# A decoder in one launch: one expert step taken up after two batches' routing, and its inner products queued in two groups

## The chip, the cores and the metric

The kernel runs on one core of a Trainium2 chip. The metric is the device time of one execution in microseconds (us); lower is better. Everything is in float32 except some small counting and quantised products in bfloat16.

## The reference, cut to what matters

Input x is 4 batches of 256 tokens with 256 features; a context of 4 x 1601 rows goes with it. Six sublayers follow each other, each ending in a residual and a layer norm: windowed attention, cross attention over the context, a quantised gated network, a causal attention with 16 heads, a linear cross attention with a gate, and last a mixture of eight experts. The change is about that last one:

```python
logits = 30 * tanh(x @ w_gate / 30)          # x is 1024 x 256, w_gate 256 x 8
probs = softmax(logits)
_, idx = top_k(probs, 2)
weights = probs * one_hot(idx).sum(-2)
for e in range(8):                            # w1, w3: 256 x 512, w2: 512 x 256
    h = silu(x @ w1[e]) * (x @ w3[e])
    out = out + h @ w2[e] * weights[:, e:e+1]
x = layernorm(x + out)
```

Each token needs two of the eight experts.

## The kernel before, in words

**Order.** The function `decoder` does not emit instructions as it goes. Each call records an operation with its inputs, outputs, assumed durations and a priority (`at_prio`) in a `Loom`. At the end, `weave` takes the operations one by one: among those whose inputs are done and whose buffers have room, the one that can start earliest by the planner's own durations goes next, and the priority breaks ties. So the order on every engine is written out by that planner, and the chip then runs each engine's queue strictly in that order, waiting where an input is late. A `piece` is a group of TensorE instructions that the planner places as one.

**Routing.** The expert sublayer does not run all tokens through all experts. For each batch, `route` finds the two experts of each token, counts how many tokens each expert has so far (`nxt`), and GpSimd scatters each token's row, with its gate and its slot, into a list in DRAM that is sorted by expert (`lists`, `scatter`). The last batch, batch 3, is routed in two halves of 128 tokens.

**Steps.** The work on the lists is done in steps of 128 rows of one expert. Which expert and which rows a step takes is known only on the chip: `tile_table` computes it with some 25 small VectorE instructions from the counts in `nxt`, and writes a table `tab` of expert numbers and row numbers. There is one table behind the routing of three batches (five steps), one behind that and the first half of the last batch (two more), and one at the end (16 steps, of which 13 always run and 3 only if the counts call for them). `EARLY` holds how many full steps the counts guarantee at each point, whatever the tokens choose.

**One step** (`expert_tile`, line 1436 and after), with the names used below, k being the number of the step in order:

- fetch: SyncE reads the row number from the table and loads 128 rows, `xg`, from `lists` (129 KB, line 1443).
- weights: SyncE reads the expert number and loads `wt`, w1 and w3 of the expert, in two transfers of 512 KB (line 1455). There are four `wt` buffers.
- T: TensorE transposes `xg` in two instructions of the program; ScalarE or VectorE copies the result to `xgT`.
- W: 16 products of `wt` with `xgT`, eight for w1 (first group, here Wa) and eight for w3 (second group, Wb). A product shows as two MATMUL records in the profile.
- ScalarE takes the tanh of the first group into `eh`. VectorE multiplies it with the first group (`eh<-eh,bank`), and then with the second group (`eh<-bank,eh`).
- Y: four products of `eh` with `w2e`, the resident w2 of all experts.
- VectorE scales the result (`ey`) and computes slot numbers; GpSimd scatters the rows to `yd` in DRAM. The last two steps are added up in PSUM with one-hot matrices (`pick`) instead, on top of the residual and of what `yd` holds (`entry`, `back`), and `finish` normalises and writes the output.

The buffers `xgT`, `eh` and `ey` of the steps lie in a pool, `p6`, of the scope `work`, which opens only when the scope `causal` is closed, that is when the causal attention of the last batch is done.

**The end of the routing.** `l1_attention` of batch 3 yields its two halves one after the other, each followed by `l1_cross` and `route`; the tables and the steps are recorded between them:

```python
if b == B - 1:
    at_prio(8)
    n = EARLY[ts[0]]
    tab, taken = tile_table(n, taken)
    for i in range(n):
        expert_tile(i, tab, level)
```

`ts[0]` is 0 for the first half (and for whole batches) and 1 for the second. `level` counts how many routings a step has to wait for: a fetch of a step is ordered only behind the scatters of lower levels.

## Time and profile before

| what | value |
|---|---|
| median of 3 runs | 690.63 us (690.26 to 690.64) |
| the profiled execution, its own time | 690.3 us |
| span of its profile, first to last instruction | 688.6 us |
| TensorE busy | 656.5 us, 95% of the span |
| VectorE, ScalarE, GpSimd busy | 444.0, 296.2, 120.7 us |
| mean granted TensorE clock | 0.985 of full speed |
| DMA | 85.36 MB, mean 124 GB/s |

The 1.7 us between the profiled execution's time and its span lie outside the first and last instruction. The times in the profile are from this one execution; its own time is 0.3 us under the median of the runs. An engine's busy share is an average over stages with different limits, and idle time of an engine that nothing waits for costs nothing. All helper calls of VectorE, ScalarE and GpSimd have one line, 408, and all products line 271, so rows are told apart by their tiles. "PE" is TensorE, "PEld" its weight loads, "DVE" VectorE, "ACT" ScalarE, "POOL" GpSimd, "SP" SyncE.

### The profile page before, as it was taken

The page shows a single profiled execution, that of the slowest core. Times are in us where ns is not written, and L with a number is a line of the kernel's source. Part 1 is how long each engine was busy: PE and PEld are TensorE (multiplying, and loading weights), DVE is VectorE, ACT ScalarE, POOL GpSimd, SP SyncE. Part 2 cuts the span into 40 slices and gives each one's busy share as a digit, 9 for nine tenths or more (in the row PEclk, how much of TensorE's full clock was granted, in tenths as well). Part 3 has the DMA queues.
Part 4 walks back from the last instruction along what each step waited for, and adds up shares of the span by engine and source line. Part 5 has one row for each costly group of instructions (what it writes and reads, how often), then busy time and mean ns, then how long its engine had stood idle before and what let it go on. Part 6 is the DMA issues. An engine that isn't in the chain of part 4 may idle for free.

```text
span 688.6 us, 12316 instructions
## 1 busy us (share of the span) xinstructions
PE 656.5 (95%) x4385; PEld 524.3 (76%) x4389; DVE 444.0 (64%) x1152; ACT 296.2 (43%) x930; POOL 120.7 (18%) x166
## 2 busy tenths in 40 slices
PE   9999999999999999999989999999997899999992
PEld 6778788678877777777667677777765799899991
DVE  6899887433526844464699997777688466434353
ACT  4779766211132423334347777656445312111101
POOL 3331132122300000000022101141203213121102
PEclk9999999999999999999999999999999899999996
DMA  9932121537998422000010340000000582895432
GB/s 307 363 96 63 45 66 40 177 100 236 335 340 307 146 96 96 0 1 1 1 54 1 105 142 1 1 32 1 31 1 21 207 277 73 295 339 217 146 130 69
DMA packets 62463, 85.36 MB, mean 124 GB/s; under 512 B 4462, under 2 KB 45812, under 8 KB 62388
## 3 DMA queue, kind: packets, MB, share of 16 engines
q1 hardware_dynamic: 60756, 79.96, 34.9%
q0 software_dynamic: 1632, 4.48, 1.8%
q8 instruction: 38, 0.62, 0.4%
q14 instruction: 37, 0.30, 0.1%
HBM read 67.29 MB, written 17.13 MB: 123 GB/s over the span
## 4 chain that ended last, share of the span: by engine, by line
PE 83%; DVE 10%; ACT 4%; POOL 1%; issue 1%; ACTq 0%; POOLq 0%; DVEq 0%
PE bank L271 74%; PE bank L278 9%; ACT at L408 3%; DVE at L408 2%; DVE nm L408 2%; DVE x L408 1%; POOL rstd L408 1%; DVE st L408 0%; DVE h L408 0%; DVE fm L408 0%; DVE as L408 0%; DVE kf L408 0%; ACT fm L408 0%; DVE back L408 0%; DVE bank L408 0%
## 5 line engine op out<-in xcount | busy, mean ns | idle before, releaser
L408 ACT ACTIVATE at<-at,nm 128x128 f32<-128x128 f32 (+1 forms) x256 | 106.4, 419 | 22.6 <-DVE nm L408 21.7
L271 PE MATMUL bank<-xgT,wt 128*128 128x128 f32 x640 | 75.9, 280 | 0.6 <-DVE xgT L408 0.5
L271 PEld LDWEIGHTS bank<-xgT,wt 128*128 128x128 f32 x640 | 75.2, 196 | 1.7 <-DVE xgT L408 0.8
L278 PE MATMUL bank<-ident,at 128*128 128x128 f32 (+1 forms) x440 | 61.4, 277 | 2.0 <-DVE at L408 1.8
L278 PEld LDWEIGHTS bank<-ident,at 128*128 128x128 f32 (+1 forms) x440 | 50.7, 142 | 14.2 <-issue 7.1
L271 PE MATMUL bank<-V,aT 128*128 128x256 f32 (+1 forms) x240 | 55.1, 380 | 0.6 <-DVE o L408 0.6
L271 PE MATMUL bank<-KT,qT 128*128 128x512 f32 (+1 forms) x128 | 54.7, 554 | 0.0
L271 PEld LDWEIGHTS bank<-V,aT 128*128 128x128 f32 (+1 forms) x240 | 45.3, 190 | 10.5 <-issue 3.6
L271 PE MATMUL bank<-kf,V 128*128 128x256 f32 (+1 forms) x208 | 50.0, 382 | 1.1 <-DVE kf L408 1.1
L408 POOL TENSOR_SCALAR rstd<-mv 128x2 f32<-128x2 f32 (+1 forms) x26 | 5.8, 222 | 258.5 <-DVE mv L408 186.2
L408 DVE TENSOR_REDUCE nm<-at 128x4 f32<-128x512 f32 (+1 forms) x64 | 50.6, 809 | 0.4
L271 PE MATMUL bank<-wkv,KT 128*128 128x256 f32 (+1 forms) x208 | 49.6, 382 | 0.0
L408 ACT ACTIVATION_READ_ACCUMULATOR at<-at,nm 128x1 f32 x256 | 48.6, 190 | 0.0
L271 PEld LDWEIGHTS bank<-kf,V 128*128 128x128 f32 (+1 forms) x208 | 38.6, 190 | 7.2 <-DVE kf L408 2.3
L271 PEld LDWEIGHTS bank<-wkv,KT 128*128 128x128 f32 (+1 forms) x208 | 38.0, 186 | 6.9 <-issue 1.0
L408 ACT COPY aT<-bank 128x512 f32<-128x512 f32 (+2 forms) x58 | 30.6, 554 | 26.6 <-PE bank L278 25.8
L408 ACT ACTIVATE eh<-bank 128x512 f32<-128x512 f32 x20 | 11.9, 597 | 66.5 <-PE bank L271 66.5
L408 DVE TENSOR_REDUCE m<-bank 128x1 f32<-128x512 f32 (+1 forms) x32 | 20.5, 640 | 29.7 <-PE bank L271 29.7
L408 DVE TENSOR_TENSOR at<-at,rs 128x512 f32<-128x512 f32 (+1 forms) x44 | 38.4, 873 | 1.0
L408 POOL TENSOR_TENSOR at<-at,rs 128x512 f32<-128x512 f32 (+1 forms) x20 | 22.8, 1141 | 87.9 <-DVE rs L408 80.7
L408 ACT ACTIVATE fm<-bank 128x512 f32<-128x512 f32 (+2 forms) x33 | 17.8, 550 | 46.6 <-PE bank L271 46.1
L271 PE MATMUL bank<-w2e,eh 128*128 x160 | 37.8, 380 | 0.0
(268 smaller groups left out, 1243.2 us busy)
## 6 DMA issues: line engine op xcount, KB each, us to landing
wt<-in_w SPq DMA_DIRECT2D x40, 512.0 KB, 5.0
lists<-h SPq DMA_DIRECT2D x6, 1548.0 KB, 17.9
KT<-in_ctxT SPq DMA_DIRECT2D x6, 1024.0 KB, 6.9
V<-in_ctx SPq DMA_DIRECT2D x6, 1024.0 KB, 6.0
w2e<-in_w SPq DMA_DIRECT2D x8, 512.0 KB, 8.7
KT<-in_ctxT SPq DMA_DIRECT2D x6, 577.0 KB, 5.1
V<-in_ctx SPq DMA_DIRECT2D x6, 512.0 KB, 4.2
xg<-lists SPq DMA_DIRECT2D x20, 129.0 KB, 4.2
```

What stands on the lines that cost most here:

```text
L271: lambda: self.nc.tensor.matmul(real(o), real(lhsT), real(rhs), start=real(start), stop=stop, **kw)
L278: fns.append(lambda: self.nc.tensor.transpose(real(o), real(x), real(ident)))
L408: return getattr(engine, method)(*[real(x) for x in args], **{k: real(x) for k, x in kw.items()})
```

## The change

There are two edits.

First, `EARLY` gets a third entry: how many full steps the counts guarantee behind the first two batches. By the formula that is one: 2 x 512 token-expert pairs less 8 x 127, divided by 128 and rounded up. The guaranteed steps are now 1, 4 and 2 in place of 5 and 2, so their sum, and the 16 of the last table, stay the same. The loop makes a table and its steps from batch 2 on (`b >= B - 2`): one step is recorded before batch 2 is routed, with a table of its own, and it is ordered only behind the scatters of batches 0 and 1.

Second, the 16 products W of a step are recorded as two pieces of eight, first group and second group, with half the assumed duration each, in place of one piece. The instructions are the same; the planner may now put other TensorE work between the groups, and it sees the first group end earlier.

```diff
-    EARLY = [-(-(2 * n - NE * (P - 1)) // P) for n in (3 * S, T - P)]
-    EARLY[1] -= EARLY[0]
+    EARLY = [-(-(2 * n - NE * (P - 1)) // P) for n in (2 * S, 3 * S, T - P)]
+    EARLY = [EARLY[0], EARLY[1] - EARLY[0], EARLY[2] - EARLY[1]]
...
         h = pool.tile((P, EI // P, P), F32, "eh")
         pa = [bank((P, EI // P, P)), bank((P, EI // P, P))]
-        with piece(3.52, [h], what="tile"):
-            for j in range(2):
+        for j in range(2):
+            with piece(1.76, [h], what="tile"):
                 for m in range(EI // P):
                     for c in range(2):
                         mm(pa[j][:, m], wt[:, j, c, m * P : (m + 1) * P], xgT[:, c, :], c == 0, c == 1)
...
-            if b == B - 1:
+            if b >= B - 2:
                 at_prio(8)
-                n = EARLY[ts[0]]
+                n = EARLY[b - B + 2 + ts[0]]
                 tab, taken = tile_table(n, taken)
                 for i in range(n):
                     expert_tile(i, tab, level)
```

## The prediction

> **What bounds the kernel now.** I read the page first, parts 1 and 4, for what carries the span.

> ```profile
> PE 656.5 (95%) x4385; PEld 524.3 (76%) x4389; DVE 444.0 (64%) x1152; ACT 296.2 (43%) x930; POOL 120.7 (18%) x166
> ...
> PE 83%; DVE 10%; ACT 4%; POOL 1%; issue 1%; ACTq 0%; POOLq 0%; DVEq 0%
> ```

> TensorE is the bound, and the change adds no product to it and takes none away. So it can only win or lose where TensorE stands still or runs slowly: 32 us in all, of which some 13 lie behind its last product. Then the stretches (busy us of PE, PEld, DVE, ACT, POOL, then clock, DMA share, GB/s) show where.

> ```profile
> 480.00:500.00 20.00, 19.97 (x128) 15.70 (x127) 12.07 (x41) 10.13 (x35) 5.01 (x6) 1.00 0.08 27
> ...
> 540.00:560.00 20.00, 17.93 (x128) 16.64 (x123) 9.44 (x55) 4.94 (x14) 4.78 (x6) 0.91 0.88 317
> 560.00:580.00 20.00, 20.00 (x156) 19.12 (x155) 10.91 (x39) 3.87 (x10) 3.13 (x5) 1.00 0.41 133
> ```

> Routing ends and the steps begin in 540 to 560: TensorE loses 2 us there and part of its clock. From 560 to 660 it has almost no gap. The timeline of TensorE gives the places:

> ```profile
> 544.11 0.51 PE L271 MATMUL bank<-wgate,xt 128*128 128x8 f32 x4
> 544.47 0.42 PE L278 MATMUL bank<-ident,xg 128*128 128x128 f32 x2
> 546.96 0.41 PE L278 MATMUL bank<-ident,x 128*128 128x128 f32 x2 [2.07 <-DVE ix L408]
> 547.20 5.37 PE L271 MATMUL bank<-xgT,wt 128*128 128x128 f32 x32
> 552.40 0.17 PE L271 MATMUL bank<-hotb,ahead 128*128 128x8 bf16 x1
> ...
> 579.31 3.73 PE L271 MATMUL bank<-xgT,wt 128*128 128x128 f32 x32
> 582.88 1.89 PE L271 MATMUL bank<-w2e,eh 128*128 x8
> ...
> 595.74 0.38 PE L278 MATMUL bank<-ident,xg 128*128 128x128 f32 x2
> 596.63 3.84 PE L271 MATMUL bank<-xgT,wt 128*128 128x128 f32 x32 [0.52 <-DVE xgT L408]
> ```

> After T0 TensorE stands, because the next item in its queue is the transpose of batch 3's second half, whose norm is late; W0 stands behind that transpose although its inputs are there (`xgT` was copied by 545.37). And W0 then takes 5.20 us from start to start, where W5 takes 3.57 (579.31 to 582.88). The clock says why:

> ```profile
> 546.00:548.00 2.00, 1.04 (x10) 1.07 (x11) 1.17 (x8) 0.37 (x1) 0.36 (x1) 1.00 1.04 399
> 548.00:550.00 2.00, 2.00 (x13) 2.00 (x12) 0.00 (x0) 0.08 (x1) 0.00 (x0) 0.56 1.05 378
> 550.00:552.00 2.00, 2.00 (x13) 2.00 (x13) 0.00 (x0) 0.52 (x1) 0.00 (x0) 0.59 1.06 380
> ```

> So the standstill costs twice. All intervals below are from start to start, since the printed ends of products overlap: pair T 0.22 (two pairs took 0.44, 554.32 to 554.76), W 3.57, a group 1.785, Y 1.73 (582.88 to 584.61), route product 0.46 (573.33 to 573.79).

> **The change, part by part.** The built program's queues show what moves; up to batch 3's second half TensorE's order is unchanged.

> *The early table* adds 25 rows on VectorE, each like the table rows at 528.91 to 539.46 (0.13 to 0.20 us): some 4.2 us. They stand between batch 1's ranking (`row`, 489.57) and batch 3's first residual sum. VectorE idles there 1.78 (before 493.49), 2.26 (before 497.67) and 0.70 us, together 4.74. Walking the queue, the softmax slips by 0.3 to 0.4 us, its product is only wanted at 498.15, and the sum at 497.67 still waits for TensorE. Cost 0. Without this cover the rows would hit the next wait of TensorE for a norm (1.08 us before 502.46) one to one; I keep 0 to 0.4, no gain possible.

> *The early fetch and weights.* SyncE reads the table, loads 1 MB of weights and 129 KB of rows at about 498, when DMA moves next to nothing; nothing else stands in its queue until the next table's reads near 540. The scatters that the fetch waits for are issued by 495.2. Cost 0. GpSimd's queue keeps its order.

> *Where the step runs.* Its buffers open only with the end of the attention, so T0 stays behind the route product at 544.11. What the early step buys is that T0 and the weights wait for no late table, and that the planner queues T0, T1, Wa of step 0, then the late transpose, then Wb. T0 ends 544.69, T1 544.91; `xgT` is copied as before by 545.37, W0a starts 545.45 (0.54 us of standing still stays) and ends 547.24. The norm's chain on VectorE, with one 0.42 us copy of `xgT` ahead of it, is ready by 547.06, so the transpose no longer waits. Of the old standstill (546.96 - 544.69 = 2.27) 0.54 remains: gain 1.73.

> *The clock.* The slow W0 cost 5.20 - 3.57 = 1.63 us. The drop came behind a break of 2.4 us between products (544.57 to 546.96, only transposes in it). A break of 1.76 us (transposes at 500.70, products again at 502.46) had none, clock 1.00. The new break is 0.9, so I take the full 1.63 as gained; bounds 0 and 1.63. [...] This trace shows no such drop behind a break under 2 us.

> *The end of the last table's chain.* The ranking of the last half moves ahead by some 9 us, because fewer W stand before it, so its fetch comes well before T7. T8's copy is no longer waited for: 596.63 - 595.96 = 0.67 gained, and W7's 0.23 us wait for weights (591.86 to 592.09) goes.

> *The two groups* have a price. Before, the product Y of a step stood at least one Y or one other W behind its own Wb. Now several Y stand straight behind their own Wb with only a few pairs T between. Y needs VectorE's second multiplication, and that needs Wb:

> ```profile
> 588.18 1.89 PE L271 MATMUL bank<-w2e,eh 128*128 x8
> 588.38 0.69 DVE L408 TENSOR_TENSOR eh<-bank,eh 128x512 f32<-128x512 f32 x1 [0.47 <-PE bank L271]
> ```

> Wb was over at 588.18, VectorE began 0.20 later and took 0.69; from VectorE's end to a product is 0.15 (the norm ended 546.81, its transpose began 546.96). So Y cannot start before 1.04 us behind its Wb. The queue of the new program has these places: Y4, Y6, Y17 with two pairs between (wait 1.04 - 0.44 = 0.60 each), Y8, Y11, Y14 with three (0.38 each), Y2 with a route product and two pairs (0.14). At Y4 some ten small rows of the last table stand ahead of the multiplication on VectorE, 0.3 more. Together 1.80 + 1.14 + 0.14 + 0.30 = 3.38. TensorE is the bound there, so all of it shows. Another 0.10 falls on the transpose of `o` behind W1a.

> *The tail.* In the new queue the last step's four `pick` pairs follow each other, where two of them stood apart. VectorE then has four batches' statistics within the last 2.6 us of products. Walking its rows (two statistics 0.73, scale 0.54, GpSimd's root 1.0 a batch) the last ScalarE row ends 4.85 us behind the last product, before 4.6 (674.83 to 679.44): cost 0.25.

> **Sum.** Gained: 2.27 + 1.63 + 0.67 + 0.23 = 4.80. Lost: 0.54 + 0.10 + 3.38 + 0.25 = 4.27. Net 0.5 us less, on the profiled execution 690.3 - 0.5 = 689.8. That execution lies 0.3 us under the median 690.63, so 690.1 as a median. A measurement of this kernel can tell about 0.2% (1.4 us) from no change, so this is no change that can be told.

> **The rivals.**

> *The output products do not wait.* If Y found its inputs ready, the 3.38 would not be paid: 690.1 - 3.4 = 686.7. For it: 560 to 660 has next to no gaps now, and the same instructions run. Against it: in TensorE's new queue nothing but pairs T stands between, and the rows of 588 give 1.04. Half of it is easily possible.

> *The output products wait longer.* Same seven places: if one more VectorE row (an `ey` of 0.48, or a first multiplication of 0.69) stands ahead of the second multiplication, as the small rows do at Y4, each wait grows by it: 7 x 0.69 = 4.8, so 694.9. From 0.28 us more a place the kernel is slower by over 1.4. For it: ScalarE's tanh and the first multiplication need 1.6 of the group's 1.785 us, so there is little room. Against it: in VectorE's new queue, `ey` and the slots stand ahead of the second multiplication at these places, but end before the Wb does, except at Y4.

> *The change does not do what it says.* The early step is not run early, only its inputs come early. That is already in the sum; if the standstill at 545 stayed whole too, because T1's rows land late (fetches of `xg` take 2.2 to 6.6 us, and T1 is issued as late as T0 was), 3.4 us of the gain would go: 693.5.

> **How the numbers follow.** The sum's own case, net within 1.4 us of nothing, gets 0.48, with 689.3 to 691.9 as its own range: a quarter to a half of the 3.4 either way. The case without waits, whole or in good part (from 689.2 down to 686.7), 0.29. Longer waits 0.13, reaching 694.9 but mostly 692 to 693.5, and the standstill that stays 0.10 at 693.5. Leaving out about 1 in 10 at each end gives 687.2 to 692.8.

> **What would show it.** Right: between the two first T and the late transpose a Wa; no clock under 0.9 in 546 to 552; W0's halves 1.8 us each; the ranking of the last half near 568; no wait before W8; six waits of 0.4 to 0.6 us (and one of 0.9) for VectorE's `eh` ahead of `w2e` products, 0.1 at Y2; PE busy some 19.4 of 20 us in stretches that had 20.00; 25 more VectorE rows and no longer wait at 502. Wrong: Y's without waits, a clock drop elsewhere, a wait for `xg` or `wt` in the first steps, or a tail over 5 us behind the last product.

## The result and the profile after

The median of the changed kernel was 690.07 us (14 runs, 688.33 to 690.82), that of the kernel before 690.46 us in the same comparison (14 runs, 688.42 to 692.31). The ratio is 0.9995 with a 95% interval of 0.9984 to 1.0006: no change that can be told, as forecast (690.1). Timed again among the experiments, on another chip, the ratio was 0.9978 (0.9964 to 0.9993). Put together, weighted by their intervals, that is 0.9989 (0.9980 to 0.9998), or 0.8 us less: at most a gain of a little over a us.

The page of after, first its busy times, then its chain of waits:

```profile
PE 656.9 (95%) x4389; PEld 522.3 (76%) x4389; DVE 447.3 (65%) x1179; ACT 295.9 (43%) x929; POOL 120.8 (18%) x166
...
PE 82%; DVE 11%; ACT 4%; issue 1%; POOL 1%; DVEq 0%; ACTq 0%; POOLq 0%
```

TensorE bounds the kernel as before; a hundredth of the chain went over to VectorE. The stretches say where (columns as in the prediction):

```profile
540.00:560.00 20.00, 19.68 (x148) 17.90 (x144) 12.53 (x63) 4.84 (x14) 4.86 (x7) 1.00 0.77 267
560.00:580.00 20.00, 18.74 (x143) 17.61 (x142) 12.27 (x56) 3.50 (x9) 5.65 (x7) 1.00 0.42 142
```

At the routing's end TensorE is busy 19.68 us instead of 17.93, at full clock. The stretch behind it, which had no gap, now has 1.26 us of them. The timeline shows both sides of the bargain (TensorE, and of VectorE the one row ahead of the last product):

```profile
544.91 0.64 PE L278 MATMUL bank<-ident,xg 128*128 128x128 f32 x4
545.87 2.05 PE L271 MATMUL bank<-xgT,wt 128*128 128x128 f32 x16 [0.32 <-ACT xgT L408]
547.76 0.38 PE L278 MATMUL bank<-ident,x 128*128 128x128 f32 x2
547.98 1.95 PE L271 MATMUL bank<-xgT,wt 128*128 128x128 f32 x16
...
577.93 1.99 PE L271 MATMUL bank<-w2e,eh 128*128 x8 [1.26 <-DVE eh L408]
...
588.84 0.69 DVE L408 TENSOR_TENSOR eh<-bank,eh 128x512 f32<-128x512 f32 x1 [1.30 <-issue]
589.58 1.99 PE L271 MATMUL bank<-w2e,eh 128*128 x8 [0.35 <-DVE eh L408]
```

T0 and T1, W0a, the late transpose, W0b: the transpose no longer waits, and 0.52 us of the standstill is left (545.87 less 544.91 and two pairs of 0.22). Further on Y4 and Y6 wait for `eh`, straight behind their own Wb and two pairs. At Y6, Wb is over at 588.64, VectorE begins its second multiplication 0.20 us later, and Y starts at 589.58, 0.94 us behind Wb.

**A measure for the rest.** In what follows, the *stops* of a trace are the time from the start of the route product near 544 us to the end of the last product, counted from start to start as in the prediction, less what the products take there at full clock, 125.59 us (before: 544.11 to 674.83 is 130.72, with 5.13 of stops in it). The *end* is the time from the last ScalarE row to the end of the span. The part ahead of the route product is left out, because the order there is the same in all these kernels apart from the rows of the early table, and still it ended anywhere from 543.0 to 545.4 us.

| kernel | ratio to before (95% interval) | stops, us | end, us |
|---|---|---|---|
| before, 4 traces | 1 | 5.1, 4.8, 6.3, 4.4 | 9.1, 8.8, 8.7, 8.6 |
| after, 2 traces | 0.9995 (0.9984 to 1.0006), 0.9978 (0.9964 to 0.9993) | 4.7, 4.7 | 9.3, 9.5 |
| table_only, table_again | 0.9936 (0.9915 to 0.9957), 0.9967 (0.9956 to 0.9979) | 3.0, 3.0 | 8.8, 9.2 |
| groups_only | 1.0028 (1.0009 to 1.0047) | 6.4 | 9.8 |
| first1 | 0.9968 (0.9956 to 0.9980) | 3.9 | 9.3 |
| ends1 | 0.9973 (0.9958 to 0.9987) | 2.6 | 10.1 |
| t22 | 0.9999 (0.9981 to 1.0016) | 5.6 | 9.3 |
| halves | 0.9969 (0.9955 to 0.9983) | 3.1 | 9.6 |
| fill | 0.9984 (0.9969 to 1.0000) | 4.3, of which 1.8 are the extra products | 8.9 |

### The profile page after: what moved, and what is told of

It reads as the page before. It is cut to its first block, busy times and chain, and to the rows that moved or that the text cites. A ratio compares the mean times of both kernels' runs of the same rounds, so it can differ in the third digit from the quotient of the medians.

```text
span 688.7 us, 12347 instructions
## 1 busy us (share of the span) xinstructions
PE 656.9 (95%) x4389; PEld 522.3 (76%) x4389; DVE 447.3 (65%) x1179; ACT 295.9 (43%) x929; POOL 120.8 (18%) x166
## 4 chain that ended last, share of the span: by engine, by line
PE 82%; DVE 11%; ACT 4%; issue 1%; POOL 1%; DVEq 0%; ACTq 0%; POOLq 0%
PE bank L271 73%; PE bank L278 9%; ACT at L408 3%; DVE at L408 2%; DVE nm L408 2%; DVE x L408 1%; DVE st L408 1%; DVE eh L408 1%; POOL rstd L408 1%; DVE h L408 0%; DVE fm L408 0%; DVE as L408 0%; DVE kf L408 0%; ACT fm L408 0%; DVE bank L408 0%
## 5 line engine op out<-in xcount | busy, mean ns | idle before, releaser
L408 ACT ACTIVATE at<-at,nm 128x128 f32<-128x128 f32 (+1 forms) x256 | 106.4, 418 | 22.6 <-DVE nm L408 21.7
L271 PEld LDWEIGHTS bank<-xgT,wt 128*128 128x128 f32 x640 | 74.8, 192 | 1.5 <-ACT xgT L408 0.6
L271 PE MATMUL bank<-xgT,wt 128*128 128x128 f32 x640 | 75.4, 275 | 0.3 <-ACT xgT L408 0.3
L278 PE MATMUL bank<-ident,at 128*128 128x128 f32 (+1 forms) x440 | 61.4, 277 | 2.0 <-DVE at L408 1.8
L278 PEld LDWEIGHTS bank<-ident,at 128*128 128x128 f32 (+1 forms) x440 | 50.8, 142 | 14.2 <-issue 7.1
L271 PE MATMUL bank<-V,aT 128*128 128x256 f32 (+1 forms) x240 | 55.1, 380 | 0.6 <-DVE o L408 0.6
L271 PE MATMUL bank<-KT,qT 128*128 128x512 f32 (+1 forms) x128 | 54.7, 554 | 0.0
L271 PEld LDWEIGHTS bank<-V,aT 128*128 128x128 f32 (+1 forms) x240 | 45.2, 190 | 10.6 <-issue 3.6
L271 PE MATMUL bank<-kf,V 128*128 128x256 f32 (+1 forms) x208 | 50.0, 382 | 1.1 <-DVE kf L408 1.1
L408 POOL TENSOR_SCALAR rstd<-mv 128x2 f32<-128x2 f32 (+1 forms) x26 | 5.8, 222 | 257.2 <-DVE mv L408 193.6
L408 DVE TENSOR_REDUCE nm<-at 128x4 f32<-128x512 f32 (+1 forms) x64 | 50.6, 807 | 0.4
L271 PE MATMUL bank<-wkv,KT 128*128 128x256 f32 (+1 forms) x208 | 49.6, 382 | 0.0
L408 ACT ACTIVATION_READ_ACCUMULATOR at<-at,nm 128x1 f32 x256 | 48.4, 189 | 0.0
L271 PEld LDWEIGHTS bank<-kf,V 128*128 128x128 f32 (+1 forms) x208 | 38.5, 190 | 7.3 <-DVE kf L408 2.3
L271 PEld LDWEIGHTS bank<-wkv,KT 128*128 128x128 f32 (+1 forms) x208 | 37.9, 186 | 7.0 <-issue 1.0
L408 ACT COPY aT<-bank 128x512 f32<-128x512 f32 (+2 forms) x58 | 30.7, 554 | 26.5 <-PE bank L278 25.8
L271 PE MATMUL bank<-w2e,eh 128*128 x160 | 38.6, 384 | 2.3 <-DVE eh L408 2.0
L408 ACT ACTIVATE eh<-bank 128x512 f32<-128x512 f32 x20 | 11.9, 598 | 66.5 <-PE bank L271 62.7
L408 DVE TENSOR_REDUCE m<-bank 128x1 f32<-128x512 f32 (+1 forms) x32 | 20.5, 639 | 29.7 <-PE bank L271 29.7
L408 DVE TENSOR_TENSOR at<-at,rs 128x512 f32<-128x512 f32 (+1 forms) x44 | 38.4, 872 | 0.9
L408 POOL TENSOR_TENSOR at<-at,rs 128x512 f32<-128x512 f32 (+1 forms) x20 | 22.9, 1143 | 88.3 <-DVE rs L408 81.1
L408 ACT ACTIVATE fm<-bank 128x512 f32<-128x512 f32 (+2 forms) x33 | 17.9, 551 | 45.9 <-PE bank L271 45.4
```

What stands on the lines that cost most here:

```text
L271: lambda: self.nc.tensor.matmul(real(o), real(lhsT), real(rhs), start=real(start), stop=stop, **kw)
L278: fns.append(lambda: self.nc.tensor.transpose(real(o), real(x), real(ident)))
L408: return getattr(engine, method)(*[real(x) for x in args], **{k: real(x) for k, x in kw.items()})
```

## The experiments

My theory was that of the prediction: the early table wins some 4 to 5 us at the routing's end, and the two groups pay most of it back where Y stands straight behind its own Wb.

### The early table without the groups

The edit to after, for `table_only` and, the same kernel once more, `table_again`:

```diff
-        for j in range(2):
-            with piece(1.76, [h], what="tile"):
+        with piece(3.52, [h], what="tile"):
+            for j in range(2):
```

> Kernel after with the 16 products W of a step as one piece again; only the early step and its table stay. In TensorE's queue no output product Y stands straight behind its own second group any more; each has at least another Y (1.73 us) in between, more than the 1.04 us that its input needs. Theory (the gain at the routing's end is real and the two groups pay it back): of the 2.27 us standstill 0.54 stays, the clock's 1.63, W8's 0.67 and W7's 0.23 are gained, nothing is lost at the Y's and the end is as before: 4.3 us less than before, about 686.2 us, ratio 0.994. Rival 1 (the gain is eaten by something else that the early table brings, such as the 0.45 us by which the trace of after runs late from 488 us on, or a later last table): 687.5 to 690. Rival 2 (the early table brings nothing without the groups, for T1 and the transpose of the last half's second norm then stand in another order): the standstill of 2 us is back and the clock falls again, 690 us.

> The kernel table_only once more (early table, products W in one piece), for more runs and a second trace. Its first trace had 3.0 us of stops between the route product at 543 and the last product, where the two traces of before had 5.1 (with a clock drop at W0) and 4.8 (without), and an end shorter by 0.1 to 0.4. Theory (what the early table gains stays if no Y stands behind its own second group): 2 to 2.5 us less than before by the traces, up to 4 by the first runs, ratio 0.994 to 0.997. Rival (the first runs were lucky in where the clock fell): ratio 0.998 to 1.000.

Measured: 687.13 us against 690.43 (0.9936), then 688.71 against 690.48 (0.9967). The stops were 3.0 us in both traces. No Y waits; the longest of TensorE's waits in this stretch are these, from the first trace (what waited, for what, us in all, times, longest):

```profile
PE bank L271 <- ACT xgT L408: 0.6, 2, 0.3
PE bank L278 <- PE bank L278: 0.4, 1, 0.4
PE bank L278 <- issue: 0.4, 1, 0.4
```

The early table alone is faster than before, by 1.4 to 5.9 us at the ends of the two intervals. The two ratios differ by more than their intervals explain well. The six runs of the first had a mean granted clock of 0.9918, the twelve of the second 0.9894; 0.0024 of 690 us is 1.7 of the 2.1 us between them, so the second, 2.3 us less than before, is the safer figure. The kernel has stops of its own that I had not counted: the pairs T2, T3, T4 stand in one row between two short pieces of work, and each of the last two starts 0.82 us behind the one before instead of 0.22 (the second and third line). What in TensorE's queue holds them up I did not take apart; after them W's run again without a gap. So the theory's 4.3 us less is an upper value, and about 2 us less is what the traces give (3.0 against the mean 5.15 of before). Rival 2, that the early table needs the groups, is out.

### The groups without the early table

`groups_only` is before with the other half of the change, the two pieces:

```diff
-        with piece(3.52, [h], what="tile"):
-            for j in range(2):
+        for j in range(2):
+            with piece(1.76, [h], what="tile"):
```

> Kernel before with the 16 products W of a step as two pieces of eight; no early step, no table of its own. TensorE's queue has T0, W0a, then the late transpose, then W0b, and further on the same seven places as the kernel after where Y stands straight behind its own second group with only pairs T between. Theory: the break before the late transpose becomes about 0.9 us, so the standstill's 1.7 us and the clock's 1.6 us are gained here too, the waits of the Y's cost the 4.1 us that the trace of after shows, W8's wait is gone or not (0 to 0.7): 690.5 to 691.2 us, the same as before or 0.7 us more. Rival (the groups cost nothing): 687 us. Rival (without the early step there is no gain, as its inputs come late): 693.5 to 694.6 us.

Measured: 692.96 us, 1.0028 (1.0009 to 1.0047): 1.9 us slower, more than I expected, and the groups do cost. The waits of the Y's are those of after to 0.01 us (1.42, 0.51 and 0.50 at Y4, Y6 and Y17). What I had wrong is the standstill, in the timeline of TensorE of groups_only:

```profile
547.41 0.46 PE L271 MATMUL bank<-xgT,wt 128*128 128x128 f32 x2 [1.20 <-DVE top L408]
548.18 0.44 PE L278 MATMUL bank<-ident,x 128*128 128x128 f32 x2 [0.31 <-DVE x L408]
```

Without the early step its weights are asked for at 541.7 and 542.3 us, and the second of the two transfers takes 5.0 us and lands at 547.3. W0 starts its first product just behind that, at 547.41 (the row names VectorE, but the products read nothing of `top`). The order is not quite that of after either: only this one product (two records) stands ahead of the late transpose, which then waits for its own input. Of the standstill some 2.0 us remain, 1.4 ahead of the first product and 0.55 behind it. That answers the prediction's third rival from the other side: most of it is filled only if the weights come early. That the weights set the start at 547.41 is read from the times alone.

### One step in two groups, and the two ends

`first1` keeps after's order at the routing's end, `ends1` also splits the last two steps:

```diff
-        for j in range(2):
-            with piece(1.76, [h], what="tile"):
-                for m in range(EI // P):
+        whole = [[0], [1]] if len(made) < 1 else [[0, 1]]     # ends1: len(made) in (0, 18, 19)
+        for js in whole:
+            with piece(1.76 * len(js), [h], what="tile"):
+                for j, m in [(j, m) for j in js for m in range(EI // P)]:
```

> Kernel after, but only the first step's products W are two pieces; all other steps have one piece of 16. The early table, the early step, the order T0 T1 W0a, late transpose, W0b are as after. Behind the other steps' second groups another step's Y stands ahead of the own one again. Theory: the waits of the Y's (4.1 us with the 0.10 that each waiting Y takes longer) go and nothing else changes, so 690.1 less 4.1 is 686.0 us, 686.0 to 686.6 if the new order finds a wait of its own. Rival (the Y waits are not on the path that sets the end; what they cost comes back later): 689 to 690 us.

> Kernel first1 with the last two steps in two groups as well, so that W19b stands between Y18 and the four pairs of pick, where first1 lost 1.5 us to VectorE's ey of step 18. Theory: the stops between the route product and the last product fall from first1's 3.95 us to 2.5, of which 1.4 are the wait of Y5: 1.5 us less than first1, about 687.4 us, ratio to before 0.994 to 0.996, as good as table_only or better by half a us. Rival (the end is set by the statistics and the last rows, not by the products): as first1, ratio 0.997.

Measured: first1 688.98 us (0.9968), ends1 688.62 (0.9973). The theory's 4.1 us less than after did not come; the stops fell by 0.8 only. All seven waits of after are gone, and two new ones stand in the trace: Y5 loses 1.44 us and the four pairs of `pick` lose 1.49, as they come straight behind Y18. The one at Y5, in the timeline of first1 (GpSimd, VectorE, TensorE):

```profile
580.54 0.96 POOL L1291 DMA_INDIRECT yd<-ey,slots  x1 [2.68 <-DVE slots L408]
...
584.88 0.16 DVE L408 SCALAR_TENSOR_TENSOR slots<-xg,spare 128x1 int32<-128x1 f32 x1 [3.90 <-issue]
585.15 0.68 DVE L408 TENSOR_TENSOR eh<-bank,eh 128x512 f32<-128x512 f32 x1
...
585.89 1.99 PE L271 MATMUL bank<-w2e,eh 128*128 x8 [1.28 <-DVE eh L408]
```

The scatter issued at 580.54 took 4.3 us to land, which makes 584.84; VectorE's next `slots` row starts at 584.88, and the second multiplication of step 5 is queued behind it. At the `slots` row before it is the same (576.90 and 3.1 us to landing make 580.0; the row starts at 580.03). So the buffer of the slot numbers is a wait that the planner, with its assumed landing time, puts ahead of the multiplication. In ends1 the wait at `pick` is gone, as expected, and the one at Y5 is 1.72. Its stops are the least of all, 2.6 us, but its end is the longest, 10.1 us, and so it is no faster than table_only.

### The planner told of the short pairs

`t22` is after with a pair T assumed at 0.22 us:

```diff
-        with piece(0.35, [xgT], ins=[tab], what="tile"):
+        with piece(0.22, [xgT], ins=[tab], what="tile"):
```

> Kernel after with one number of the planner changed: a pair T is assumed to take 0.22 us, as the trace has it, in place of 0.35. The instructions are the same and every step has two groups; but the planner now sees that three pairs don't cover the 1.04 us that Y's input needs, and puts half of another W (1.78 us) ahead of it everywhere. Theory: no Y waits, the gain at the routing's end stays: 686.0 to 686.8 us. Rival (the split into groups costs by itself, by the tighter buffers for the second multiplication or by a busier VectorE, wherever Y stands): 688.5 to 690.5 us.

Measured: 690.74 us, 0.9999 (0.9981 to 1.0016): the rival. One Y still waits for `eh`, 0.29 us at 589.68; all others have half of another W ahead of them. But that half now stands straight behind its own pairs T and waits for its `xgT`: 0.24 to 0.45 us at five places, 1.6 us in all, and 0.5 more as each such half takes 0.10 longer. T2 to T4 lose 1.5 as in table_only. The stops are 5.6 us, more than after's. My reading is that a piece of half the size must have some cover ahead of it, either for `eh` or for `xgT`, and cutting the W's in two leaves half as much of it; the pairs T are too short to be any.

### Half of the multiplication

`halves` leaves after's order as it is and splits the second multiplication:

```diff
-        k.vector.tensor_tensor(h, pa[1], h, ALU.mult)
+        def twice():
+            for m in (slice(0, 2), slice(2, 4)):
+                nc.vector.tensor_tensor(real(h)[:, m], real(pa[1])[:, m], real(h)[:, m], ALU.mult)
+
+        k.op({"DVE": (0.608, 0.693, twice)}, [h], [pa[1], h], what="tensor_tensor")
```

> Kernel after with VectorE's second multiplication (128 x 512, 0.69 us) as two instructions of 128 x 256, so that the first two products of Y can start when half of eh is there. The order on all engines stays that of after. Theory (the waits of the Y's are on the path, and their length is VectorE's work behind the second group): the first half is done 0.27 us earlier (a 128 x 256 row on VectorE takes 0.42), so each of the six waits of Y4, Y6, Y8, Y11, Y14, Y17 is 0.27 us shorter and Y2's 0.14 goes: 1.7 us less than after, 688.4 us. Rival (the waits are given back further on, by the end's VectorE work or by a late transfer): 690 us as after.

Measured: 688.64 us, 0.9969, where after on the same chip had 689.74 and 0.9978. The stops are 3.06 against after's 4.73: 1.67 us less, where 1.7 was expected. At Y6, for one, in the timeline of TensorE of halves:

```profile
587.14 0.60 PE L278 MATMUL bank<-ident,xg 128*128 128x128 f32 x4
587.82 1.99 PE L271 MATMUL bank<-w2e,eh 128*128 x8
```

From T to Y it is 0.68 us, 0.44 for the pairs and 0.24 of waiting, where it was 0.50. So the waits shrink with VectorE's work behind the second group, at the places forecast: that work is the price of the groups. In the medians 1.1 of the 1.67 us shows, with intervals of about 1 us either way.

### The break and the clock

`fill` is before with eight products in the standstill that nobody needs; `before_again`, `before_third` and `before_fourth` are before unchanged, `after_again` is after:

```diff
             for c in range(2):
                 turn(pt[:, c, :], xg[:, c * P : (c + 1) * P], ident)
+            if not made:
+                idle = bank((P, EI // P, P))
+                for m in range(8):
+                    mm(idle[:, m % 4], ident, ident, True, True)
```

> Kernel before with eight extra products behind T0 (the identity times itself, into a bank that nobody reads; 8 of the 128 x 128 kind that W is made of, at 0.22 us each 1.8 us in all). They lie inside the standstill of 2.27 us, so the late transpose and W0 start when they did, 546.96 and 547.20 in the trace of before. Only the break in TensorE's products changes, from 2.4 us to some 0.7. Theory (the break brings the clock down, and every execution pays for it): W0 takes 3.57 in place of 5.20 us, 1.6 us less than before in all: 688.8 us, ratio 0.9977, mean clock 0.002 higher. Rival (the fall of the clock at this place is a matter of single executions, as the mean clocks of the runs of before and after, 0.9885 and 0.9883, suggest, or comes whatever TensorE does): same as before, ratio 0.999 to 1.001; W0 in the trace may take either time. Rival (the extra products reach past the standstill): up to 0.3 us more.

> The kernel before unchanged, for a second trace. Theory: standstill of 2.3 us before the late transpose and W0 at 5.2 us as in the first trace. Rival (the drop of the clock there is a matter of single executions): W0 at 3.6 to 4.5 us.

> The kernel before once more, for a third trace. The first had W0 at 5.20 us with the clock at 0.56 to 0.59, the second 3.57 at full clock, both behind the same break of 2.4 us. Expected: one or the other, nothing between (a drop lasts 3 to 4 us, or is absent); without the drop W7 waits about 1 us for its weights, with it 0.2.

> As the run ahead of it: W0 at 5.2 us or at 3.6, and the wait of W7 for its weights long where W0 is short.

> The kernel after unchanged, timed on the chip that the variants run on, and a second trace of it. Expected by the theory: ratio to before 0.9985 to 1.0005; W0's two groups 1.8 us each again, waits of the Y's as in the first trace (0.5 to 1.4 us); if clock drops are a matter of single executions, one may show here in 546 to 560 or the drops at 345 to 355 and 535 to 540 may be missing.

Measured: fill 690.06 us against 691.60, 0.9984 (0.9969 to 1.0000). First the third trace of before, then the second, from the late transpose on:

```profile
546.52 0.41 PE L278 MATMUL bank<-ident,x 128*128 128x128 f32 x2 [2.07 <-DVE ix L408]
546.77 5.36 PE L271 MATMUL bank<-xgT,wt 128*128 128x128 f32 x32
551.97 0.17 PE L271 MATMUL bank<-hotb,ahead 128*128 128x8 bf16 x1
```

```profile
546.40 0.41 PE L278 MATMUL bank<-ident,x 128*128 128x128 f32 x2 [2.07 <-DVE ix L408]
546.65 3.74 PE L271 MATMUL bank<-xgT,wt 128*128 128x128 f32 x32
550.22 0.17 PE L271 MATMUL bank<-hotb,ahead 128*128 128x8 bf16 x1
```

The same wait of 2.07 us before the same transpose, and W0 takes 5.20 us once and 3.57 once. Of the four traces of before, the first and third have the drop, the second and fourth do not. Of the ten traces of kernels with a shorter standstill, none has it here. In fill W0 takes 3.57 us behind the filled standstill, and the mean clock of its runs is 0.98975 against 0.98852 for before on that chip: 0.0012 of 690 us is 0.85 us of clock, about half of what one drop takes. That is a rough measure: the same kernel differs by 0.0024 between table_only and table_again.

The traces' record of the clock shows where the two pairs of traces differ. Ahead of the last product the drops start at 346.84, 534.57 and 548.22 us in the first trace of before and at 347.35 and 535.09 in that of after. They are 187.73 us apart in both traces, 55 times 3.413, and then 13.65 in before, 4 times 3.413; each lasts 3.41 us at a clock of 0.50. Cut into stretches of that length, counted from a trace's own drops, the times around W0 (columns as above) are, for the third trace of before and then for the second:

```profile
543.41:546.82 3.41, 1.34 (x11) 1.08 (x11) 2.40 (x13) 0.69 (x3) 1.77 (x3) 1.00 1.03 390
546.82:550.24 3.42, 3.42 (x18) 3.42 (x18) 0.28 (x2) 0.37 (x1) 0.00 (x0) 0.50 1.04 372
```

```profile
544.77:548.19 3.42, 1.79 (x16) 1.82 (x17) 1.74 (x12) 0.42 (x2) 0.84 (x3) 1.00 1.03 379
548.19:551.60 3.41, 3.41 (x34) 3.40 (x33) 1.10 (x7) 0.75 (x2) 0.00 (x0) 1.00 1.06 392
```

In the third trace the whole standstill lies in one stretch, TensorE is busy for 1.34 us of it (1.34 in the first trace too) and the clock of the next is 0.50. In the second trace the cut goes through the standstill, 1.79 us are left (some 1.8 in the fourth) and the clock stays at 1.00. So in these four traces the drop at W0 came where the standstill lay whole in one stretch. That this decides it is my reading: no run moved the cuts. The two theories were both half right.

After_again came out at 0.9978, a little below the 0.9985 to 1.0005 that I expected. Two more expectations failed. With W0 short I expected W7 to wait long for its weights and with W0 long not; it lost 0.23, 1.00, 0.72 and 0.73 us in the four traces, with the drop in the first and third. The link is not there; the typical wait is 0.7.

## Why the prediction was right, step by step

The forecast was no change, from 4.80 gained and 4.27 lost. By the traces, stops fell from 5.15 (mean of four) to 4.73 (two), and the end grew by 0.56 (mean of two against mean of four): nothing either way, to 0.2 us. The timings say 0.3 and 1.5 us less. Half a us to 1.6 us of this is in no row that I compared; it may lie ahead of the route product, where executions differ by 2 us. That stays open. The mechanism was right, gains at the routing's end against waits of the Y's. That the median came out at 690.07 where 690.1 was forecast is luck: the clock's term, W7's, the groups' and the tail's were each off by 0.3 to 0.8 us, and the errors nearly cancel.

*The standstill*: 2.27 in all four traces of before, 0.52 left in after, 0.54 forecast. Right, and groups_only points to the early weights as what it takes.

*The clock*: W0's groups took 1.89 and 1.78 us at full clock, as forecast. The term of 1.63 was mis-sized: it took one execution for all. By the four traces it is worth about half, 0.8 us: the middle of my bounds of 0 and 1.63, not their upper end. The mean clocks of after's own timed runs, 0.9883 and 0.9891, do not show it plainly against 0.9885 for before, and the longer end lowers them too. Two readings in this part of the prediction were wrong. The break between products is 2.6 us (544.57 to 547.20); 2.4 reaches only to the late transpose. And the length of the break between products does not tell by itself whether a drop follows: in the trace of after there is no product but transposes for 3.30 us (518.13 to 521.43), longer than the break at W0, and the clock stayed at 1.00. With the transposes counted TensorE is busy for 1.97 us from 517.99 to 521.41.

*W8's and W7's waits*: gone, as forecast. W8's is 0.67 or 0.68 in each trace of before; W7's is 0.7 rather than 0.23, so the change gained 0.4 more here than I had put down. In three of the four traces of before a pair of `pick` near the end also waits, for 0.26 to 0.55 us, and in after none does; this was in no term.

*The groups*: the step that decided, and right in kind and place: seven Y's wait, at the seven places named. Forecast and measured: Y2 0.14 and 0.14, Y6 and Y17 0.60 and 0.50, Y8, Y11 and Y14 0.38 and 0.29, Y4 0.90 and 1.41; together 3.38 and 3.43. At Y6 the 1.04 us was 0.94, because Y followed the end of VectorE's row (589.53) by 0.05 us where I had taken 0.15. Each of the seven then takes 1.83 instead of 1.73 us, which I had not seen coming, so the price is 4.1. Y4 was the term that failed, because VectorE had a stop of its own there (timeline of after, GpSimd and VectorE):

```profile
575.85 0.96 POOL L1291 DMA_INDIRECT yd<-ey,slots  x1 [2.69 <-DVE past L408]
...
577.00 0.28 DVE L408 TENSOR_REDUCE rowt<-past 128x16 f32<-128x128 f32 x1 [1.08 <-PE bank L278]
577.20 0.68 DVE L408 TENSOR_TENSOR eh<-bank,eh 128x512 f32<-128x512 f32 x1
```

A table row waited 1.08 us, with the multiplication queued behind it. It reads no product, so the releaser named is not the cause; it starts 0.19 us behind the end of GpSimd's scatter (575.85 and 0.96 make 576.81). The same pair of rows has the same 1.08 us in the second trace of after, in halves, groups_only, table_only and table_again, each time 0.13 to 0.19 us behind the scatter. No run took the scatter away, so that it is the cause is not shown.

*The early table's rows*: cost 0, as forecast; the residual sum still waits for TensorE, and TensorE's wait for the norm near 502 is 1.1 us as before. The route product of after begins 0.44 us later than in the first trace of before, but 0.20 earlier in the second trace of after than in the second of before.

*The transpose of `o`*: no wait, 0.10 forecast. *The tail*: the last ScalarE row ends 4.57 and 4.56 us behind the last product in after and 4.57 to 4.63 in before, so VectorE's statistics cost nothing and the 0.25 was wrong. But behind that row it takes longer in all seven traces in which the four pairs of `pick` follow each other (9.3 to 10.1 us, mean 9.55) than in the seven others (8.6 to 9.2, mean 8.88). The first of the four output transfers is then issued 3.1 us ahead of the end of that row in place of 4.0, and the four lie closer together. That they hold each other up is argued, not shown.

*The rivals.* Output products that do not wait: halves and t22 show that only another order would give that, and another wait took its place there. Longer waits: only at Y4. The standstill that stays: not in after, but most of it in groups_only.

## What to carry to other kernels

When a piece of work is cut so that more can be put in between, list for each consumer what then lies between it and its producer, and price it by the measured chain: half a W covers `eh` or `xgT` for one neighbour only, and where TensorE is the bound each uncovered consumer cost its full 0.3 to 0.5 us here. Test the two halves of a change alone: here the early table by itself (0.9936 and 0.9967) beats the kernel that also has the groups. A clock drop seen in one execution is a term with a probability; look at several traces before counting it in full (here it came in two of four).

## What the runs showed of the hardware

Cut into stretches of 3.413 us as above, up to the last product, the five that are followed by a drop in the first traces of before and after hold 0.90, 0.97, 1.34, 1.76 and 1.77 us of TensorE work, transposes counted, and all others at least 1.94. The 1.79 and some 1.8 us of the second and fourth traces of before had no drop behind them.
